# A graph network layer on one core: eight tiles that SyncE fetched row by row are gathered by GpSimd

## The chip, the cores and the metric

One core of a Trainium2 chip runs the whole kernel. The metric is the time of one execution on the device in microseconds, as the median of several runs. The engines are TensorE (PE, with its weight loads as PEld), VectorE (DVE), ScalarE (ACT), GpSimd (POOL) and SyncE (SP). A suffix q (SPq, DVEq) means the engine's sequencer: waits, register work and DMA issues.

## The reference

There are 12500 nodes with 128 features each and 400000 edges, sorted by destination. Cut to what matters:

```
rbf  = exp(-(distances[:, None] - centers)**2 / (2 * width**2))          # 50 centers up to 10.0
cut  = 0.5 * (cos(pi * distances / CUTOFF) + 1) * (distances <= CUTOFF)
W    = (silu(rbf @ fw1 + fb1) @ fw2 + fb2) * cut[:, None]                # per edge
messages = (h[src] @ pw + pb) * W
agg  = segment_sum(messages, dst)
y    = h + silu(agg @ mw1 + mb1) @ mw2 + mb2
out  = layernorm(x + y)
```

Edges longer than the cutoff of 10.0 contribute nothing, and most edges here are longer.

## The kernel before, in words

The program is written in the order in which it is to be issued: a manual schedule, in which a modelled clock decides how instructions of several activities are interleaved. Each engine works off its own instructions in that order, and waits on semaphores for its operands.

**Lists.** The edge list is cut into seven chunks of rows of 128 partitions. For each chunk VectorE shifts the near edges of a row to its front (`pack`, lines 508 to 512 and 502), puts them in lines (`columns`, L477 and L479), and GpSimd scatters the lines into a list `packed` in DRAM (L487). `unpack` reads the list back on SyncE (L805), separates sources, destinations and lengths (L823 to L853), transposes them on TensorE and copies the sources to `srci` (L891), one column for 128 edges. The lengths go to `near_d` in DRAM (L880).

**Quads.** The near edges make 139 quads of 512 edges, numbered q, each of four tiles of 128 edges, numbered j. QB gives the first quad of each chunk: 0, 13, 24, 46, 69, 91, 114. For each quad:

- `fetch` (L1026) gathers the projected rows `h[src] @ pw + pb`: one indirect DMA on GpSimd's queue per tile (L1032), 128 rows of 512 bytes, from the table `proj` in DRAM into a buffer `got`. The first 12 quads are gathered from `x` itself and projected afterwards, because `proj` isn't written yet.
- `radial` (L1046) loads the lengths of two quads on SyncE's queue, broadcast over the partitions (`d<-near_d`). ScalarE makes the radial basis of them (L1073, L1074), TensorE and ScalarE the first layer (`ph`, L1082; silu, L1088), TensorE the second (L1096, L1099).
- `message` (L1103) multiplies that with the gathered rows on VectorE (L1110). This is what gives the quad's buffer back.
- `place` (L1122) makes on VectorE a matrix that is the cutoff weight where an edge's destination meets a column; `sum_up` (L1142) multiplies it with the messages on TensorE, and `add` (L1165) adds the sums into `aggT` at the quad's base.

**Buffers.** There are 13 buffers `quad` and 8 buffers `x` for gathered rows, also used for other things. `place_of` gives each quad its buffer: at first all 21, from quad 63 on only nine, with ever fewer turns in between (at the end each buffer comes back after four quads). A gather waits until the message of the quad that had the buffer before is done.

**Gathers in order.** `fetches` (L435) puts gathers on GpSimd's queue as long as indices and buffers are there by the program's own model. It keeps a modelled time of GpSimd, `pool[0]`, and from it `there_at[q]`, when a quad will have landed; the modelled clock that paces the list-building (`pack_until`) goes by both.

**Single rows.** For the eight quads in `SINGLY` the first tile (j = 0) isn't gathered by GpSimd. `unpack` turns the sources into byte offsets, `at_row` (L905, once for each chunk that has such a quad), and appends 128 single rows per quad to a list `singles`. `one_by_one` (L1009), called once per quad of the main loop at L1470, issues some of these on SyncE's queue: a load of 32 offsets into registers (L1018), then for each row a plain DMA of 512 bytes (L1022) into `dl_0`, a keep tile with four places. `message` then takes the first tile from `dl_0` (L1108) and the other three from the gathered buffer (L1110), in two instructions:

```
            if j or q not in SINGLY:          # fetches, L442
                pool[0] += 1.29
...
            if q in SINGLY and j == 0:        # fetch, L1029
                continue
...
        if q in SINGLY and a == 0:            # message, L1106
            nc.vector.tensor_mul(msg[:, 0, :], pu_of[q][:, :H], alone.pop(q))
            a = 1
```

**Nodes.** From quad 70 on, finished columns of `aggT` go through the node layers (L1173 to L1176, L324, L327), the layer norm (L1192 to L1229) and out to DRAM (L170), in groups of node tiles set by quad number. The last groups come behind the last quad.

Of the kernel before, what the change touches and what calls it, by code (L numbers as in the profile page):

```python
# [65 lines left out]
CLEAR_C = 2  # L66
PACK_US = 1.5
EARLY_US = 7
SINGLY = (22, 45, 62, 67, 86, 102, 118, 133)
A_ROW = .58  # L70
AT_ONCE = 32
FROM_BANK = 3
# [8 lines left out]
def kernel(  # L81
# [342 lines left out]
    def before_it(q):  # L424

        return max((m for m in range(q) if place_of(m) == place_of(q)), default=-1)
# [8 lines left out]
    def fetches(until, most):  # L435

        while fetched[0] < QT * min(most, known[0]) and pool[0] <= until:
            q, j = divmod(fetched[0], QT)
            fetch(q, table=x if q < FROM_X else None, js=(j,))
            if j == 0:  # L440
                pool[0] = max(pool[0], summed.get(before_it(q), 0.0))
            if j or q not in SINGLY:  # L442
                pool[0] += 1.29
# [351 lines left out]
    def unpack(c):  # L795
# [105 lines left out]
        yield 0  # L901
        mine = [q for q in SINGLY if QB[c] <= q < QB[c + 1]]
        if mine:
# [105 lines left out]
    def one_by_one():  # L1009

        row_at[0] = max(row_at[0], clock[0] - 8.0)
        while singles and row_at[0] < clock[0]:
            row_at[0] += A_ROW
            q, e, i = singles.pop(0)
            if e == 0:
                alone[q] = dl_0[:, SINGLY.index(q) % 4, :]
            if e % AT_ONCE == 0:
# [8 lines left out]
    def fetch(q, idx=None, table=None, js=range(QT)):  # L1026
        got = quad_sb[place_of(q) if q >= 0 else 0]
        for j in js:
            if q in SINGLY and j == 0:  # L1029
                continue  # L1030
# [72 lines left out]
    def message(q, js=(0, QT)):  # L1103
        msg = own(q, "msg", 0)
        a, b = js
        if q in SINGLY and a == 0:  # L1106
            assert q in alone and all(s[0] != q for s in singles)
# [539 lines left out]
```

## Time and profile before

| | |
|---|---|
| median of 3 runs | 727.36 us (726.96 to 729.21) |
| the profiled execution | 731.18 us, of which the span in the trace 729.3 |
| TensorE, VectorE busy | 591.7 us (81%), 561.8 us (77%) |
| GpSimd, ScalarE busy | 532.4 us (73%), 402.7 us (55%) |
| DMA queues' share of 16 engines | q1 22.0%, q0 (GpSimd's) 19.6% |
| mean granted TensorE clock | 0.926 |

The profile is of one execution. Its page has the busy time of each engine, the span in 40 slices with the busy share in tenths, the chain of work that ended last, and the groups of instructions. A group's row has the source line, engine, operation, output<-inputs and the count, then busy us and mean ns of one, then the idle time of the engine just before these instructions with what ended it. "issue" there means that the engine waited for nothing that the profile shows. A row of the instructions in order of time has the start and the duration in us, then the instruction, and in brackets the idle time before it. A row of the waits has who waited for whom, the total in us, the number of times, and the longest. Busy time does not count register, semaphore and DMA-issuing instructions; for GpSimd's indirect DMAs the work of the engine itself is counted.

### The profile page before, as it was taken

To read this page: it belongs to the slowest core of one execution; us is meant where nothing else is said; L and a number is where in the kernel's file an instruction comes from. 1 tells how busy PE (TensorE), PEld (TensorE's weight loads), DVE (VectorE), ACT (ScalarE), POOL (GpSimd) and SP (SyncE) were. 2 spreads that over 40 slices of the span, in tenths; PEclk is the share of its full clock that TensorE was granted. 3 is DMA by queue.
4 is the path that set the end of the run, shared out by engine and by line. 5 is a ranking of instruction groups with operands and counts; after the bars stand their busy time and mean duration, and the time that the engine had idled before them with its cause. 6 is when DMAs were issued, how large, how long until landed. Compare 5 with 4: busy or idle time off the path is not lost.

```text
span 729.3 us, 13631 instructions
## 1 busy us (share of the span) xinstructions
PE 591.7 (81%) x3531; PEld 463.5 (64%) x3531; DVE 561.8 (77%) x1734; ACT 402.7 (55%) x572; POOL 532.4 (73%) x569
## 2 busy tenths in 40 slices
PE   6878777797888797888788979999977878887974
PEld 5767566576656676667466757777755656565752
DVE  8897998878968998989689959768555546564774
ACT  6547634275345864536347364839644744374584
POOL 6776777777777777777777777777777777777770
PEclk9998887999989998999889998999998989999998
DMA  8995443243234333242333343434433433445242
GB/s 262 326 314 182 124 134 87 68 145 90 87 100 140 86 96 106 84 141 81 88 99 121 104 105 114 147 116 142 126 99 113 139 99 98 112 125 149 55 139 69
DMA packets 53104, 91.38 MB, mean 125 GB/s; under 512 B 13824, under 2 KB 20576, under 8 KB 53018
## 3 DMA queue, kind: packets, MB, share of 16 engines
q1 hardware_dynamic: 34610, 53.34, 22.0%
q0 software_dynamic: 17840, 36.77, 19.6%
q8 instruction: 30, 0.49, 0.3%
q14 instruction: 56, 0.46, 0.2%
q10 hardware_dynamic: 568, 0.33, 0.2%
HBM read 74.59 MB, written 15.79 MB: 124 GB/s over the span
## 4 chain that ended last, share of the span: by engine, by line
DVE 25%; POOL 18%; PE 17%; issue 16%; DMA 15%; ACT 4%; DVEq 2%; SPq 1%; POOLq 0%; ACTq 0%
POOL quad L1032 14%; DMA quad<-proj,srci 7%; POOL x L1032 5%; DVE hot L1122 4%; PE bank L1099 4%; PE sums L1142 4%; PE ph L1082 3%; DVE aggT L1165 2%; DVE msg L1110 2%; PE bank L327 2%; DMA pair<-packed 2%; DVEq L1151 2%; DMA proj<-hp 2%; DVE r_d L502 2%; DVE quad L1122 2%
## 5 line engine op out<-in xcount | busy, mean ns | idle before, releaser
L1032 POOL DMA_INDIRECT quad<-proj,srci x421 | 400.5, 951 | 130.5 <-issue 104.9
L1099 PEld LDWEIGHTS bank<-fw_sb,s 128*128 128x128 f32 x1112 | 162.2, 210 | 67.5 <-issue 60.0
L1088 ACT ACTIVATE s<-ph 128x1024 f32<-128x1024 f32 x70 | 71.2, 1017 | 169.9 <-PE ph L1082 169.8
L1099 PE MATMUL bank<-fw_sb,s 128*128 128x128 f32 x1112 | 162.1, 293 | 0.0
L1082 PE MATMUL ph<-rbf,w_sb 102*128 102x512 f32 x278 | 141.1, 632 | 9.2 <-ACT rbf L1074 4.9
L1142 PEld LDWEIGHTS sums<-hot,msg 128*128 128x128 f32 x816 | 106.4, 196 | 55.2 <-DVE msg L1110 27.1
L1122 DVE TENSOR_SCALAR hot<-iota_n,dl,cut 128x80 f32<-128x80 f32 (+4 forms) x408 | 108.7, 343 | 24.8 <-PE sums L1142 22.0
L1142 PE MATMUL sums<-hot,msg 128*128 128x80 f32 (+4 forms) x816 | 109.5, 278 | 14.2 <-DVE msg L1110 13.9
L1096 PE MATMUL bank<-fb_b,ones_b 96*128 96x512 bf16 x139 | 56.8, 409 | 49.0 <-DVE msg L1110 24.5
L1032 POOL DMA_INDIRECT x<-proj,srci x79 | 75.3, 953 | 24.1 <-issue 20.7
L1110 DVE TENSOR_TENSOR msg<-bank,quad 128x512 f32<-128x512 f32 (+1 forms) x82 | 55.4, 676 | 41.6 <-DMA quad<-proj,srci 30.8
L1082 PEld LDWEIGHTS ph<-rbf,w_sb 102*128 102x128 f32 x278 | 50.5, 202 | 47.4 <-issue 36.7
L1165 DVE TENSOR_TENSOR aggT<-aggT,sums 128x80 f32 (+4 forms) x209 | 53.7, 257 | 27.4 <-PE sums L1142 10.7
L1073 ACT ACTIVATE rbf<-d,rbf_bias,rbf_scale 102x512 f32<-102x512 f32 x70 | 56.2, 803 | 26.5 <-DMA d<-near_d 26.4
L1032 POOL DMA_INDIRECT quad<-in_x_dram,srci x48 | 47.0, 979 | 18.7 <-issue 14.7
L327 PEld LDWEIGHTS bank<-pw_sb,xT 128*128 128x128 f32 (+1 forms) x292 | 43.5, 215 | 11.3 <-ACT xT L968 5.0
L1088 ACT ACT_TABLE_LOAD x36 | 46.2, 1283 | 0.6
L1074 ACT ACT_TABLE_LOAD x35 | 44.9, 1283 | 0.6
L327 PE MATMUL bank<-pw_sb,xT 128*128 128x128 f32 (+1 forms) x292 | 44.5, 301 | 0.8 <-ACT xT L968 0.6
L1074 ACT ACTIVATE rbf<-rbf 102x512 f32<-102x512 f32 x70 | 44.1, 630 | 1.5
L1142 PE MATMUL sums<-quad,quad 128*128 128x128 f32 (+3 forms) x296 | 42.4, 290 | 2.2 <-DVE quad L1110 1.9
L1110 DVE TENSOR_TENSOR quad<-bank,quad 128x512 f32<-128x512 f32 (+2 forms) x40 | 25.1, 631 | 24.3 <-DMA quad<-proj,srci 20.4
(268 smaller groups left out, 809.9 us busy)
## 6 DMA issues: line engine op xcount, KB each, us to landing
d<-near_d SPq DMA_DIRECT2D x70, 256.0 KB
dl<-proj SPq DMA_DIRECT2D x1024, 0.5 KB
x<-in_x_dram SPq DMA_DIRECT2D x46, 256.0 KB
quad<-proj,srci POOLq DMA_INDIRECT x421
proj<-hp SPq DMA_DIRECT2D x24, 256.0 KB
out_dram<-x SPq DMA_DIRECT2D x22, 256.0 KB
r_d<-in_edge_weight_dram SPq DMA_DIRECT2D x5, 256.0 KB
r_dst<-in_dst_dram SPq DMA_DIRECT2D x5, 256.0 KB
```

The source lines that it names most:

```text
L327: nc.tensor.matmul(to[:m, k, :], lT[:, k * P:k * P + m], w, start=False, stop=(k == a + c - 1))
L1032: nc.gpsimd.indirect_dma_start(out=got[:, j, :], out_offset=None, in_=proj if table is None else table, in_offset=bass.IndirectOffsetOnAxi ...
L1073: nc.scalar.activation(rbf[:u], d[:u], AF.Square, bias=rbf_bias[:u], scale=rbf_scale[:u])
L1074: nc.scalar.activation(rbf[:u], rbf[:u], AF.Exp, scale=-1.0 / (2.0 * width * width))
L1082: nc.tensor.matmul(ph[:, h, :], w1_sb[:2 * KR, h, :], rbf[:2 * KR], start=True, stop=True)
L1088: nc.scalar.activation(s[:, :n], ph[:, :n], AF.Silu)
L1096: nc.tensor.matmul(pu, ones_b[:, :P], bias_b["fb2"].rearrange("k j f -> k (j f)"), start=True, stop=False)
L1099: nc.tensor.matmul(pu[:, j * H:(j + 1) * H], s[:, j * P:(j + 1) * P], fw2_sb, start=False, stop=(j == QT - 1))
L1110: nc.vector.tensor_mul(msg[:, a:b, :], pu_of[q].rearrange("p (j f) -> p j f", j=QT)[:, a:b, :], got_of[q][:, a:b, :])
L1122: nc.vector.tensor_scalar(hot[:, j, :wide(q)], iota_n[:, :wide(q)], dl[:, at[0], at[1]], cut[:, at[0], at[1]], op0=OP.is_equal, op1=OP.mult)
L1142: nc.tensor.matmul(pa[:, k * W:k * W + wide(q)], msg[:, j, :], hot[:, j, :wide(q)], start=(j % n == 0), stop=(j % n == n - 1))
L1165: nc.vector.tensor_add(to, to, pa[:, k * W:k * W + wide(q)])
```

## The change

The tuple of quads whose first tile comes by single rows is emptied:

```
-SINGLY = (22, 45, 62, 67, 86, 102, 118, 133)
+SINGLY = ()
```

All 556 tiles are then gathered by GpSimd. `singles` stays empty, so `one_by_one` issues nothing, `at_row` isn't computed, and each message is one instruction. Since `fetches` counts 1.29 for each of the eight tiles more, the modelled times `pool[0]` and `there_at` grow, and the list-building instructions of the later chunks stand at somewhat other places between the quads.

## Prediction

> **What bounds the kernel now.** I read the page's shares of the span first, then the groups of GpSimd (POOL), its instructions in order of time, and last the messages of VectorE (DVE), which consume what GpSimd gathers.
>
> ```profile
> span 729.3 us, 13631 instructions
> ...
> POOL 6776777777777777777777777777777777777770
> ...
> DVE 25%; POOL 18%; PE 17%; issue 16%; DMA 15%; ACT 4%; DVEq 2%; SPq 1%; POOLq 0%; ACTq 0%
> ```
>
> By shares nothing is full: the chain that ended last passes over five engines, and GpSimd is never busier than seven tenths. But its row is the same digit from the second slice to the last but one. An engine that waits for others has an uneven row; this one looks like an engine that is always at it and loses a fixed share between its instructions. The groups of GpSimd (busy us, mean ns | idle us just before them) say so:
>
> ```profile
> L1032 POOL DMA_INDIRECT quad<-proj,srci x421 | 400.5, 951 | 130.5 <-issue 104.9 <-DVE aggT L1165 6.4 <-DMA quad<-proj,srci 5.2
> L1032 POOL DMA_INDIRECT x<-proj,srci x79 | 75.3, 953 | 24.1 <-issue 20.7 <-DMA x<-proj,srci 0.9 <-DVE aggT L1165 0.6
> L1032 POOL DMA_INDIRECT quad<-in_x_dram,srci x48 | 47.0, 979 | 18.7 <-issue 14.7 <-DVE srci L539 2.4 <-DMA proj<-hp 0.6
> L487 POOL DMA_INDIRECT packed<-line,at_i x7 | 7.0, 998 | 2.7 <-issue 1.5 <-DVE base_i L624 0.9 <-DVE aggT L1165 0.3
> ```
>
> There are 421 + 79 + 48 = 548 gathers and 7 scatters. Their idle time adds up to 130.5 + 24.1 + 18.7 + 2.7 = 176.0 us, or 0.317 us before each of the 555. In order of time (start, duration, what, idle before it) nearly every one has 0.30 or 0.31; those with more, and some that I need as marks, are:
>
> ```profile
> 7.11 1.21 POOL L1032 DMA_INDIRECT quad<-in_x_dram,srci  x1 [2.41 <-DVE srci L539]
> ...
> 71.38 0.94 POOL L1032 DMA_INDIRECT quad<-in_x_dram,srci  x1 [2.25 <-issue]
> ...
> 133.68 0.94 POOL L1032 DMA_INDIRECT quad<-proj,srci  x1 [0.30 <-issue]
> 136.37 0.94 POOL L1032 DMA_INDIRECT quad<-proj,srci  x1 [1.74 <-DVE at_row L905]
> ...
> 489.43 0.94 POOL L1032 DMA_INDIRECT quad<-proj,srci  x1 [1.08 <-DVE quad L1110]
> ...
> 549.40 0.94 POOL L1032 DMA_INDIRECT quad<-proj,srci  x1 [0.30 <-issue]
> ...
> 649.40 0.94 POOL L1032 DMA_INDIRECT quad<-proj,srci  x1 [0.30 <-issue]
> ...
> 668.22 0.94 POOL L1032 DMA_INDIRECT quad<-proj,srci  x1 [0.30 <-issue]
> ...
> 709.49 0.94 POOL L1032 DMA_INDIRECT quad<-proj,srci  x1 [0.30 <-issue]
> ```
>
> From 7.11 to 709.49 us GpSimd issues one gather behind the other. From 668.22 to 709.49 there are 33 steps: 41.27 / 33 = 1.2506 us each (0.94 of work, 0.30 between). Past its start it waited three times: 2.25 - 0.30 = 1.95 us at 71.38, 1.44 at 136.37, 0.78 at 489.43. That is all.
>
> Does the end follow from the last gather? I gave each gather its quad (a group of 512 edges) by counting, four to a quad and three where the quad is in SINGLY, and put the quad's message, the VectorE product that consumes it, beside its last gather. Quads 45, 97 and 134:
>
> ```profile
> 245.81 0.94 POOL L1032 DMA_INDIRECT quad<-proj,srci  x1 [0.30 <-issue]
> 291.97 0.55 DVE L1110 TENSOR_TENSOR msg<-bank,quad 128x384 f32<-128x384 f32 x1
> 508.15 0.94 POOL L1032 DMA_INDIRECT quad<-proj,srci  x1 [0.30 <-issue]
> 510.90 0.69 DVE L1110 TENSOR_TENSOR msg<-bank,quad 128x512 f32<-128x512 f32 x1 [1.47 <-PE bank L1099]
> 689.45 0.95 POOL L1032 DMA_INDIRECT quad<-proj,srci  x1 [0.30 <-issue]
> 692.97 0.69 DVE L1110 TENSOR_TENSOR quad<-bank,quad 128x512 f32<-128x512 f32 x1 [1.31 <-DMA quad<-proj,srci]
> ...
> 714.38 0.29 DVE L1110 TENSOR_TENSOR quad<-bank,quad 128x128 f32<-128x128 f32 x1 [0.76 <-issue]
> ```
>
> The lead of the gathers is 46.2 us at quad 45, 2.75 at quad 97, and stays near 3 up to quad 134, whose message waits for its data. VectorE's waits between 560 and 640 us (total, times, longest) show the same:
>
> ```profile
> DVE msg L1110 <- DMA quad<-proj,srci: 15.3, 6, 4.1
> DVE quad L1110 <- DMA quad<-proj,srci: 12.1, 8, 2.1
> ```
>
> So GpSimd has the stock, the consumer eats it up by about 505 us, and from there each message waits for GpSimd. Up to quad 134 **the gather queue sets the end**; the rest, from 692.97 to 729.3, is a tail of 36.3 us behind it.
>
> **The change part by part.** Eight quads lose their row-wise first tile. Removed on SyncE and VectorE:
>
> ```profile
> L1022 SPq DMA_DIRECT2D dl<-proj x1024: 224/228/405, 82.7 to 666.7; - x171
> L905 DVE TENSOR_SCALAR at_row<-f_src x6: 207/208/346, 79.9 to 445.3; 44x128 int32<-44x128 f32 x2, 46x128 int32<-46x128 f32 x2, 22x128 int32<-22x128 f32 x1, 54x128 int32<-54x128 f32 x1
> 685.72 0.29 DVE L1108 TENSOR_TENSOR msg<-bank,dl 128x128 f32<-128x128 f32 x1
> 687.08 0.56 DVE L1110 TENSOR_TENSOR msg<-bank,quad 128x384 f32<-128x384 f32 x1 [1.06 <-DMA quad<-proj,srci]
> ACT rbf L1073 <- DMA d<-near_d: 26.4, 9, 5.3
> ```
>
> - SyncE loses 1024 x 0.228 = 233 us of issuing. What stood behind the rows in its queue, the broadcast loads of the lengths (d<-near_d), goes out earlier, so up to 26.4 us of ScalarE's nine waits can go. VectorE loses 6 x 0.208 = 1.2 us and, with one product in place of two, 8 x (0.29 + 0.56 - 0.69) = 1.3 us. I count all this at nothing: the consumer before 505 us has a stock of gathers in front of it, and past 505 us it waits for GpSimd. Being earlier only lengthens those waits. If that cover were gone, it would be worth the second rival's price.
> - Added: 8 gathers, 548 becoming 556. All eight lie before quad 134, in GpSimd's queue ahead of everything that follows. Seven go in at 1.2506: **+8.75 us**.
> - The eighth, quad 22's, comes just before the wait at 136.37. GpSimd waits there for quad 24's indices, the first of the third list, written by this copy:
>
> ```profile
> 135.85 0.25 DVE L891 CAST srci<-bank 128x88 int32<-128x88 f32 x1 [0.42 <-PE bank L886]
> 488.47 0.69 DVE L1110 TENSOR_TENSOR quad<-bank,quad 128x512 f32<-128x512 f32 x1
> 422.94 0.29 DVE L479 TENSOR_TENSOR line<-r_d,bank 128x136 int32<-128x136 int32 x1
> 428.43 0.99 POOL L487 DMA_INDIRECT packed<-line,at_i  x1 [0.30 <-DVE aggT L1165]
> ```
>
>   The profile names at_row, the instruction right behind the copy, as the releaser; what the gather reads is srci. The queue stands still for 1.44 us, and a gather takes 1.25. It fits whole: **0**. If the indices came 1.4 us sooner it would cost 1.25.
> - The wait of 0.78 us at 489.43 is for a buffer (quad 94's), given back by quad 90's message of 488.47. Five added gathers lie ahead of it, of which four count: GpSimd gets there 5.0 us later and finds the buffer free, if that message is not 4.2 us later as well: **-0.78**.
> - Moved: the scheduler reckons GpSimd's time with 1.29 us for each gather, so the list-building instructions shift. In the changed program's order of instructions the last three scatters stand 0, 1 and 4 of the old gathers later in GpSimd's queue, and the index copies of the lists 0 to 3 messages later on VectorE. A scatter must not come before its lines: the tightest of these was ready at 423.23 and issued at 428.43, and now gets 8 gathers more ahead of it, so it waits for nothing. The last list's copy, at 445 before, is wanted by quad 114 at 588; 3 messages are some 12 us. Also nothing.
>
> Sum: 8.75 + 0 - 0.78 = **+8.0 us**. The profiled execution took 731.18 us (729.3 of span and 1.9 around it), so it would take 739.2. It lies 3.8 above the median of the runs, 727.36; on that median the forecast is **735.3 us**, 1.1% slower.
>
> The tail is taken over unchanged: the last message stands at 714.38, 4.9 us behind the last gather's start, where 2.75 was usual. There the consumer, not GpSimd, is late, by 4.9 - 2.75 = 2.1 us. If the relief of SyncE and ScalarE gave all of that back, the time would be 733.2, and 732.8 from the lowest of the runs, 726.96.
>
> **One rule of the Trainium skill weighed.** What a gather costs beside a busy VectorE is on these rows (all gathers into quads: shortest/median/longest ns; VectorE's busy us in two stretches):
>
> ```profile
> L1032 POOL DMA_INDIRECT quad<-proj,srci x421: 938/944/1344, 73.9 to 709.5; - x141
> 300.00:400.00 100.00, 88.39 (x248) 0.91 0.34 102
> 600.00:700.00 100.00, 61.13 (x205) 0.94 0.38 109
> ```
>
> Half the gathers take 944 ns or less although VectorE is busy for 88% of one stretch, and the worst takes 1344. If each added gather were a worst one, the price would grow by 8 x 0.40 = 3.2 us: 738.5. The Trainium skill, "SBUF — State Buffer", section "SBUF: two separate sides", says that a DMA issued from GpSimd starves while VectorE runs in a two-port mode, and its next section gives 620 ns alone against 3100 beside such a copy. That speaks against the change: by those figures eight gathers would cost an estimated 8 x 2.5 = 20 us more. This trace has no gather of that kind, so the sum goes by 944 ns.
>
> **The rivals.**
> 1. *Full price.* All eight gathers cost 1.25, because the waits at 136.37 and 489.43 move along with the lists and the messages: 8 x 1.2506 = 10.0, 737.4 us. For it: both waits are set by VectorE, whose order changes. Against: up to quad 22 only one 0.2 us instruction leaves VectorE, and VectorE has less to do by 489. 0.13.
> 2. *The consumer sets the pace* (other side: faster). Rows on SyncE hold back the length loads, ScalarE and then the messages; without them the messages come earlier, and the end with them. Price: at most the 26.4 us, 701 us. It decides only where GpSimd waits for buffers for longer than the 8 us added; it waited 0.78. 0.02.
> 3. *The rows slow the gathers* (no change). 1024 row transfers share the DMA engines with the gathers. Without them each gather might take its shortest, 938: busy time 522.8 us less 548 x 0.938 = 8.8 us, which pays for the whole change, 726.6. Against: from 549.40 to 649.40, with rows in flight, 80 steps take 1.2500; past the last row at 666.7 they take 1.2506. 0.03.
> 4. *Starved gathers*, the rule above: 738.5 by the worst row. 0.05.
> 5. *A shorter tail*, 733.2 as worked out: 0.07.
>
> That the change does something else is out: the changed program holds 556 gathers and no row transfer.
>
> **How the numbers follow.** The forecast, 734 to 736.5, gets the remaining 0.70. The range, 732.8 to 738.5, takes in the shorter tail, the full price and the worst row. A measurement of this kernel can tell about 0.3%, 2.2 us, from no change. Faster by more: rival 2, 0.02. Within: rival 3, 0.03. Slower: the rest, 0.95.
>
> **What would show it.** 556 gathers, again 1.25 us apart; the idle time before the first gather of quad 24 down from 1.74 to about 0.5, and no wait near 490; quad 134's last gather issued at 697.4 with its message still waiting for it; the last gather at 717.5; fewer waits of ScalarE for d, worth nothing. I am wrong if GpSimd shows waits of more than a microsecond behind quad 24, if the step is not 1.25, or if messages past quad 100 no longer wait for gathers.

## The result, and the profile after

The changed kernel takes 738.15 us in the median of 4 runs (736.08 to 739.7), the kernel before 728.29 in 4 runs on the same chip (726.96 to 730.58): a ratio of 1.0109, 95% interval 1.0073 to 1.0144, which is 7.9 us; the two medians themselves lie 9.9 us apart. Measured a second time, with other kernels beside it, it was 737.46 us against 730.51: 1.0085 (1.0056 to 1.0114), or 6.2 us, with 7.0 between the medians. So the change costs 6 to 10 us, about 1%; 8.0 had been forecast.

The page after, the busy line, GpSimd's row of the 40 slices and its largest group:

```profile
span 734.3 us, 11523 instructions
...
PE 590.1 (80%) x3531; PEld 463.1 (63%) x3531; DVE 560.6 (76%) x1720; ACT 403.9 (55%) x573; POOL 540.5 (74%) x577
...
POOL 6777777777777777777777777777777777777770
...
L1032 POOL DMA_INDIRECT quad<-proj,srci x428 | 407.4, 952 | 130.6 <-issue 104.5
```

GpSimd has 8 instructions and 8.1 us of busy time more (532.4 before) and the same flat row. The profiled execution took 736.08 us, 4.9 more than the one of before; it was the shortest of the four, and that of before, with 731.18, was longer than any of its four. In it, the first gather of quad 24 (start, duration, idle before), the last gather of quad 134 with its message, and the last gather of all:

```profile
134.12 0.94 POOL L1032 DMA_INDIRECT quad<-proj,srci  x1 [0.49 <-DVE part L910]
...
695.88 0.94 POOL L1032 DMA_INDIRECT quad<-proj,srci  x1 [0.30 <-issue]
698.93 0.69 DVE L1110 TENSOR_TENSOR quad<-bank,quad 128x512 f32<-128x512 f32 x1 [0.25 <-DMA quad<-proj,srci]
...
715.94 0.94 POOL L1032 DMA_INDIRECT quad<-proj,srci  x1 [0.30 <-issue]
```

In this execution the idle time before quad 24 has fallen from 1.74 to 0.49, with quad 22's gather ahead of it. No gather near 490 us waits any more. Between these gathers and their partners of before, the differences are -2.25 at quad 24 (134.12 - 136.37), +6.43 at quad 134 and +6.45 at the end. So the queue behind quad 24 became 8.7 us longer, and everything up to quad 24 ran 2.25 us earlier in this execution: it was 2.05 us ahead at quad 12 already, at 71.82 us, when no row transfer is out yet (the first of before is at 82.7). Behind the last gather 18.4 us are left (734.3 - 715.9), 19.8 before. Hence 8.7 - 2.25 - 1.45 = 5.0 in the span. The first of these three numbers belongs to the change, as the other runs show. The last does not: with the rows kept, the rest behind the last gather is as short (18.4 in the gathers alone). For the 2.25 no cause was found. The four kernels below without rows start quad 24 at 134.1 to 135.9 us and four with rows at 136.2 to 137.4; but among the latter is the one with only quad 22 moved, whose first row goes out at 138.4, and a kernel with ten quads by rows starts it at 133.4.

The waits of ScalarE and VectorE that SyncE's rows were suspected of (total, times, longest), from the waits of the changed kernel:

```profile
ACT rbf L1073 <- DMA d<-near_d: 3.2, 3, 1.6
DVE msg L1110 <- DMA quad<-proj,srci: 33.7, 15, 5.5
DVE quad L1110 <- DMA quad<-proj,srci: 27.9, 17, 3.6
```

ScalarE's waits for the length loads went from 26.4 us to 3.2. That is a real relief, and the kernel is slower. VectorE's waits for gathers went from 51.2 us to 61.6: what is gained ahead of a queue that sets the pace is spent waiting for it. Their rows in the kernel before:

```profile
DVE msg L1110 <- DMA quad<-proj,srci: 30.8, 15, 4.1
DVE quad L1110 <- DMA quad<-proj,srci: 20.4, 13, 2.5
```

### The profile page after: what moved, and what is told of

It is laid out like the page before. It is cut to its first block, busy times and chain, and to the rows that moved or that the text cites. A ratio compares the mean times of both kernels' runs of the same rounds, so it can differ in the third digit from the quotient of the medians.

```text
span 734.3 us, 11523 instructions
## 1 busy us (share of the span) xinstructions
PE 590.1 (80%) x3531; PEld 463.1 (63%) x3531; DVE 560.6 (76%) x1720; ACT 403.9 (55%) x573; POOL 540.5 (74%) x577
## 5 line engine op out<-in xcount | busy, mean ns | idle before, releaser
L1032 POOL DMA_INDIRECT quad<-proj,srci x428 | 407.4, 952 | 130.6 <-issue 104.5
L1082 PE MATMUL ph<-rbf,w_sb 102*128 102x512 f32 x278 | 142.8, 639 | 5.5 <-ACT rbf L1074 4.0
L1142 PEld LDWEIGHTS sums<-hot,msg 128*128 128x128 f32 x816 | 108.2, 199 | 54.4 <-issue 26.9
L1142 PE MATMUL sums<-hot,msg 128*128 128x80 f32 (+4 forms) x816 | 110.5, 280 | 14.5 <-DVE msg L1110 14.3
L1110 DVE TENSOR_TENSOR msg<-bank,quad 128x512 f32<-128x512 f32 x82 | 55.9, 681 | 39.0 <-DMA quad<-proj,srci 33.7
L1110 DVE TENSOR_TENSOR quad<-bank,quad 128x512 f32<-128x512 f32 (+1 forms) x40 | 25.9, 648 | 32.2 <-DMA quad<-proj,srci 27.9
```

The source lines that it names most:

```text
L1032: nc.gpsimd.indirect_dma_start(out=got[:, j, :], out_offset=None, in_=proj if table is None else table, in_offset=bass.IndirectOffsetOnAxi ...
L1082: nc.tensor.matmul(ph[:, h, :], w1_sb[:2 * KR, h, :], rbf[:2 * KR], start=True, stop=True)
L1110: nc.vector.tensor_mul(msg[:, a:b, :], pu_of[q].rearrange("p (j f) -> p j f", j=QT)[:, a:b, :], got_of[q][:, a:b, :])
L1142: nc.tensor.matmul(pa[:, k * W:k * W + wide(q)], msg[:, j, :], hot[:, j, :wide(q)], start=(j % n == 0), stop=(j % n == n - 1))
```

## The experiments

**The two halves of the change, each alone.** The first kernel adds the gathers and keeps the rows, which are still used; only the lines that skip the gather go:

```
-            if q in SINGLY and j == 0:
-                continue
```

> The kernel before with the eight first tiles gathered by GpSimd as well: the rows are still fetched by SyncE and still used, the order of everything else is that of before. Theory (GpSimd's queue sets the end): 556 gathers, seven of the eight added ones at 1.25 us, quad 22's hidden in the wait at 136 us, the buffer wait near 489 us gone: +8.0 us, ratio 1.011, the same as the change. Full price: +10.0, 1.0137. If SyncE's rows set the consumer's pace: the change's gathers cost more than its +8 to +10 and the removed rows give some back, so this kernel is slower than the changed one, above 740.

Measured: 737.15 us (6 runs) against 730.15, ratio 1.0096 (1.0067 to 1.0126). ScalarE's waits for d were 23.6 us, as before. Apart from the added gathers the instructions stand in the order of before, so it isn't the shifted list-building instructions that cost the time.

The second takes out the rows and adds no gather; in the first tile of the eight quads the message multiplies by ones, so that part of the result is left out:

```
 def one_by_one():
+    singles.clear()
...
-            nc.vector.tensor_mul(msg[:, 0, :], pu_of[q][:, :H], alone.pop(q))
+            nc.vector.tensor_mul(msg[:, 0, :], pu_of[q][:, :H], ones)
```

> The kernel before without the row transfers and their register loads on SyncE; the first tile of the eight quads isn't fetched by anyone, the message multiplies by a tile of ones instead (so this part of the result is left out). 548 gathers as before. Theory: no change, 0 to -1 us (the buffer wait of 0.78 at most goes), down to -2.9 if the tail gives back its lateness too; GpSimd's steps stay at 1.25. Consumer's pace: as much as ScalarE's waits for d, up to -26 us, ratio down to 0.965. Rows slow the gathers: -8.8 us, ratio 0.988, and a step shorter than 1.25.

Measured: 728.22 us (12 runs) against 730.15, ratio 0.9975 (0.9959 to 0.9991). So the added gathers are the whole cost (+7.0 us) and the removed rows give back between 0.7 and 3.0 us at best, not the 26 of the waits. ScalarE's waits for d fell to 14.3 us here, and VectorE's for gathers rose to 32.7 + 30.2 = 62.9: with no gather added, the relief is spent waiting. With gathers and without rows, the change itself was measured once more, on another chip and with the kernel before beside it:

> The changed kernel as it is, beside the others. Theory: +8.0 us on the kernel before, ratio 1.011, the same as with the rows kept (1.0096 measured there). If the rows' removal paid for something, it would lie below that, about 1.007.

Measured: 1.0085 (1.0056 to 1.0114). It can't be told from 1.0096, the gathers alone. The 0.0025 that the rows are worth by themselves is within what these intervals leave open, so whether a part of it survives in the changed kernel isn't settled.

**Is quad 22's gather free?** Once with only this one moved, once with the other seven:

```
-SINGLY = (22, 45, 62, 67, 86, 102, 118, 133)
+SINGLY = (45, 62, 67, 86, 102, 118, 133)     # e3
+SINGLY = (22,)                               # f4
```

> Only quad 22's first tile goes to GpSimd, the other seven stay with SyncE: 549 gathers. Theory: no change in time (within 0.3 us); in the profile the idle time before quad 24's first gather falls from 1.74 to about 0.5 and that gather starts no later relative to its neighbours. Full price: +1.25 us, ratio 1.0017, and the idle time there stays near 1.7.

> Seven of the eight first tiles go to GpSimd, quad 22's stays with SyncE: 555 gathers. Theory: the full change less a gather that was hidden, so the same time as the changed kernel: +8.0 us, ratio 1.011, with the wait of 1.4 us before quad 24's first gather as in the kernel before. If each added gather cost the same: 7/8 of the change's cost, 1.25 us less than the changed kernel.

Measured: 1.0011 (0.9988 to 1.0034) with only quad 22 moved, 1.0101 (1.0071 to 1.0132) with all but it: the time of the kernel before, and that of the changed one. One gather of 1.25 us is 0.17% and too small for these intervals; the profiles decide. First gather of quad 24, then any wait near 490, then the last gather, with only quad 22 moved:

```profile
136.16 0.94 POOL L1032 DMA_INDIRECT quad<-proj,srci  x1 [0.49 <-DVE at_row L905]
...
490.86 0.94 POOL L1032 DMA_INDIRECT quad<-proj,srci  x1 [2.73 <-DVE quad L1110]
...
710.93 0.94 POOL L1032 DMA_INDIRECT quad<-proj,srci  x1 [0.30 <-issue]
```

and with all but quad 22 moved:

```profile
137.43 0.94 POOL L1032 DMA_INDIRECT quad<-proj,srci  x1 [4.31 <-DVE part L910]
...
719.51 0.95 POOL L1032 DMA_INDIRECT quad<-proj,srci  x1 [0.30 <-issue]
```

With the gather the wait is 0.49 here, as in the first profile of the changed kernel, and without it 4.31. But this difference isn't the gather's alone. The second profile of the changed kernel, with the gather, has 1.73 there, as much as the kernel before without it, and the gathers alone have 2.37; first the one, then the other:

```profile
135.07 0.95 POOL L1032 DMA_INDIRECT quad<-proj,srci  x1 [1.73 <-DVE part L910]
```

```profile
137.12 0.94 POOL L1030 DMA_INDIRECT quad<-proj,srci  x1 [2.37 <-DVE at_row L905]
```

The wait is as long as it takes until the third list's indices are there, and that moment differs from one execution to the next: quad 24 starts at 134.12, 135.07, 136.16 and 137.12 us with quad 22's gather, and at 134.30, 136.37 and 137.43 without it. In each of these profiles GpSimd still waits there for longer than its usual 0.30, so the gather fits in ahead of the wait, twice with only 0.19 us to spare. GpSimd's row of gathers starts anew at that point: what stands ahead of it, an added gather or a late start, doesn't count as long as some of the wait is left; what stands behind it does.

**A double dose.** The changed kernel, with each of the eight gathers made once more, into a tile that nobody reads:

```
+            if q in AGAIN and j == 0:
+                nc.gpsimd.indirect_dma_start(
+                    out=dl_0[:, AGAIN.index(q) % 4, :], out_offset=None, in_=proj,
+                    in_offset=bass.IndirectOffsetOnAxis(ap=i, axis=0))
```

> The changed kernel with each of the eight added gathers made twice (the second into a tile nobody reads): 564 gathers. Theory: a linear price, again 1.25 us each, of which quad 22's finds only some 0.2 us of waiting left: +9.8 us on the changed kernel, ratio 1.0245 to the kernel before, and the messages past quad 97 or earlier wait for gathers. If the eight were partly hidden or the consumer set the pace: less than +6 on the changed kernel. If added gathers are starved by VectorE: more than +12.

Measured: 745.83 us (5 runs), ratio to the kernel before 1.0228 (1.0201 to 1.0254), so 16.6 us where 17.8 was expected. The price is about linear: in the table below the first seven gathers behind quad 24 add 8.7 us and the next seven 8.2. The same two marks in this kernel, and the group of the additional gathers:

```profile
135.93 0.94 POOL L1037 DMA_INDIRECT quad<-proj,srci  x1 [1.49 <-DVE part L911]
...
725.94 0.94 POOL L1037 DMA_INDIRECT quad<-proj,srci  x1 [0.30 <-issue]
```

```profile
L1034 POOL DMA_INDIRECT dl<-proj,srci x8 | 7.6, 947 | 2.4 <-issue 2.1 <-DMA quad<-proj,srci 0.3
```

Put together, from quad 24's first gather to the last of all, for each profiled execution (the rest of the span behind it in the last column):

| kernel | gathers added behind quad 24 | first to last, us | rest of the span |
|---|---|---|---|
| before | 0 | 573.1 | 19.8 |
| rows out | 0 | 573.5 | 18.5 |
| only quad 22 moved | 0 | 574.8 | 18.5 |
| gathers alone | 7 | 582.2 | 18.4 |
| all but quad 22 moved | 7 | 582.1 | 18.4 |
| changed | 7 | 581.8 | 18.4 |
| changed, again | 7 | 581.8 | 18.3 |
| double dose | 14 | 590.0 | 18.1 |

Three groups, and rows or no rows makes no difference in them. The 574.8 has its 1.7 us over 573.1 in the buffer wait at 490.86: 2.73 - 0.30 = 2.43 there, 0.78 in the kernel before.

**More rows in place of fewer.** If gathers are what costs, ten or twelve quads by single rows should be faster than eight. The modelled pace had to be quickened for the rows to fit:

```
-SINGLY = (22, 45, 62, 67, 86, 102, 118, 133)
-A_ROW = .58
+SINGLY = (22, 45, 62, 67, 86, 102, 110, 118, 126, 133)                 # f2
+A_ROW = .46
...
+SINGLY = (22, 34, 45, 56, 67, 78, 88, 98, 108, 118, 126, 133)          # f3
+A_ROW = .33
```

> Ten quads by single rows in place of eight, the two new ones late (22, 45, 62, 67, 86, 102, 110, 118, 126, 133), with the rows issued at a quicker modelled pace (A_ROW 0.46 in place of 0.58). 546 gathers. Theory: two gathers less behind quad 97, where every message waits for GpSimd: -2.5 us, ratio 0.9966. If SyncE's rows begin to hold back the consumer: 0 or slower, with messages past quad 100 no longer waiting for gathers.

> Twelve quads by single rows (22, 34, 45, 56, 67, 78, 88, 98, 108, 118, 126, 133), A_ROW 0.33. 544 gathers. Seven of them lie before quad 94 (five before), five behind it (three before). Theory with the buffer wait as a floor: GpSimd reaches quad 94 2.5 us sooner and only waits that much longer for its buffer, so the two early ones are lost and the two late ones gain: -2.5 us, ratio 0.9966, and a wait of some 3 us near 487. If only the count of gathers mattered: -5.0 us, 0.993, and no such wait. If the denser rows hold back the consumer: 0 or slower, waits of GpSimd for buffers of more than 4 us.

Measured: 767.34 us, 1.0493 (1.0458 to 1.0529), with ten, and 904.23 us, 1.2358 (1.2319 to 1.2397), with twelve. The expected -2.5 us didn't come: here the consumer falls behind, the rival that the runs with eight quads rule out there. Both the number of rows and the pace were changed, so these two runs don't tell which of them did it. The waits with ten quads, then with twelve:

```profile
ACT rbf L1073 <- DMA d<-near_d: 132.5, 31, 10.3
...
DVE two L823 <- DMA pair<-packed: 31.6, 5, 11.1
POOL quad L1032 <- DVE msg L1110: 25.3, 12, 9.6
```

```profile
ACT rbf L1073 <- DMA d<-near_d: 235.9, 39, 12.7
...
POOL quad L1032 <- DVE msg L1110: 113.5, 20, 17.7
...
DVE two L823 <- DMA pair<-packed: 60.1, 4, 23.2
```

What came late are the loads on SyncE's queue, which stand among the rows: the lengths (d) and the lists. And GpSimd, whose longest wait for a buffer in the kernel before was 1.1 us, now waits for them for 25.3 us with ten quads and 113.5 with twelve. A likely reason stands in SyncE's instructions in order of time, first with twelve quads, then in the kernel before:

```profile
505.58 12.78 SPq L1022 DMA_DIRECT2D dl<-proj  x31
518.55 0.37 SPq L170 DMA_DIRECT2D x<-in_x_dram  x1
519.02 0.53 SPq L1046 DMA_DIRECT2D d<-near_d  x1
519.66 11.34 SPq L1022 DMA_DIRECT2D dl<-proj  x26
```

```profile
513.95 3.74 SPq L1022 DMA_DIRECT2D dl<-proj  x9
...
522.07 8.29 SPq L1022 DMA_DIRECT2D dl<-proj  x17
```

One issue takes 228 ns in the median, but the stretch of 31 takes 12.78 us. A load of 32 offsets into registers is in it (L1018, 2.17 us at 510.6), so a row with what lies between costs 0.34 there; in the stretch of 17, which has such a load of 2.14 us too, 0.36, and in the nine rows without one 0.42. With its share of the load, 2.16 / 32 = 0.07, a row takes SyncE an estimated 0.41 to 0.49. At a modelled pace of 0.58 per row that leaves some room for its other work; at 0.46 little or none, at 0.33 less than none. That this is what held back the consumer is argued from these figures, not shown by a run of its own.

**An attempt to cure that.** Three kernels were to tell the pace from the count, and to take the length loads out of the rows' way: the pace alone (eight quads, A_ROW 0.46), the loads on ScalarE's queue with eight quads, and the same with ten, which was measured once more:

```
-        nc.sync.dma_start(d, v.to_broadcast([64, 2, QE]))
+        nc.scalar.dma_start(d, v.to_broadcast([64, 2, QE]))
```

> The kernel before with only the modelled pace of the rows changed, A_ROW 0.46 in place of 0.58: the same eight quads, 1024 rows and 548 gathers, but each quad's rows are put more densely among SyncE's other work. Theory: ten quads lost 37 us because rows really take some 0.4 us of SyncE each, so that at this pace the length loads behind them come late; then this kernel too is slower, by 5 to 30 us, with ScalarE's wait for d above 50 us (26.4 before). If only the number of rows mattered: no change.

> The kernel before with the length loads (d<-near_d) issued on ScalarE's queue in place of SyncE's; rows and gathers as before. Theory: GpSimd's queue sets the end, so 0 to -1 us, ScalarE's wait for d mostly gone. Rival: the 70 issues of 0.52 us are 36 us more of ScalarE's sequencer and delay the silu and with it the messages: slower by up to 36.

> Ten quads by single rows as in the earlier run (A_ROW 0.46, 546 gathers), but with the length loads on ScalarE's queue, out of the rows' way. Theory: the 37 us of that run came from the length loads behind the rows, so they go, and the two gathers less give -2.5 us against the kernel before, ratio 0.9966. If the rows hold back something else on SyncE (the lists' reads, the row transfers themselves): still slower than the kernel before by 10 us or more.

> The same kernel once more, beside a kernel before that takes its usual time: ten quads by single rows (A_ROW 0.46, 546 gathers), length loads on ScalarE's queue. Theory: the 37 us of the ten-quad run came from the length loads behind the rows in SyncE's queue; with these out of the way ScalarE hardly waits for d (132.5 us there), and two gathers less give -2.5 us, ratio 0.9966. If the rows hold back the lists' reads or the row transfers themselves instead: slower than the kernel before by 10 us or more, with VectorE waiting for the lists. If ScalarE's 70 issues of some 0.5 us cost it: slower, by up to 36 us, with GpSimd waiting for buffers.

All four ran on chips on which the kernel before itself took 1070 and 1071 us (three on one, the last on another), with a granted TensorE clock of 0.73 to 0.77 in their profiles (0.926 in the kernel before elsewhere), so they can't be set beside the runs above. Why these chips are so much slower isn't known. Against the same chip's kernel before, the ratios were 1.0268 (1.0111 to 1.0426) for the pace, 1.1137 (1.0925 to 1.135) for the loads on ScalarE, 1.2011 (1.1763 to 1.2259) for ten quads with them, and 1.2024 (1.1952 to 1.2096) for that once more. GpSimd waits long for buffers in all of them, least with the pace alone:

```profile
POOL quad L1032 <- DVE msg L1110: 134.3, 23, 20.0
```

So on such a chip denser rows cost something by themselves, and ScalarE's queue is the wrong place for the loads. How the loss with ten quads on a chip with the usual times divides into pace and count, and whether more than eight quads could pay there, stays open.

## Why the prediction was right, point by point

- **GpSimd's queue sets the end up to quad 134.** Right. One wait of GpSimd was left out of the working, 0.89 us at 32.23 before a scatter, far ahead of all that the change touches. From quad 24 to the last gather the profiles fall into three groups by the number of gathers there, with or without rows: seven more add 8.7 to 9.1 us, fourteen 16.9.
- **Seven gathers at 1.25, +8.75, less a buffer wait, -0.78.** Both terms are right; one of +0.8 is missing. From quad 24 to the end the queue grew by 8.7 us where 8.0 had been worked out. In the rows of the two profiles the buffer wait is gone, as forecast, but all the work of GpSimd behind quad 24 adds up to 440.7 us where it was 433.3: 7.4 more, of which seven gathers of 0.944 are 6.6. The other 0.8 are gathers that took longer than the usual 0.944; why there were more of them is open. The buffer wait itself differs between executions: it is 0.78 in the one of before, 2.43 in the one with only quad 22 moved, 0.38 at 487 (and 0.76 at 467) with the rows out. Seven added gathers eat up whatever it is, so this part of the cost differs with it.
- **735.3 us, most likely 734 to 736.5.** The forecast rested on a median of three runs, 727.36, and the kernel before was at 728.29 to 730.51 each time that it was measured beside others. The measured 738.15 lies inside the range but above those limits, nearer to the 737.4 of the full price: by this time alone, rival 1 would have looked better, and by the second measurement, with 7.0 us between the medians, worse. The forecast marks in the profile, 697.4 for quad 134's last gather and 717.5 for the last of all, were passed 1.5 and 1.6 us sooner: quad 24 started 2.25 us earlier, and the queue behind it grew by 0.7 more than forecast.
- **Quad 22's gather costs nothing.** Right, and for the reason given: with it GpSimd still waits at quad 24. The sign that was named for it, a wait down from 1.74 to about 0.5, is no good sign, though: it came true in the first profile and not in the second (1.73). Not seen: that the wait is a point where all executions start anew, and that its place differs by 3.3 us between them. That, and the tail, is why the two profiled executions differ by 5.0 us and not by 8.
- **What SyncE, ScalarE and VectorE lose is worth nothing.** Right to 0.25%: by itself it is worth 0.7 to 3.0 us. Where that comes from is open. It isn't saved behind quad 24: the profile with the rows out has 573.5 us from there to the last gather, 573.1 with them, and still has its buffer waits. That execution was ahead of the one of before by 2.07 us at quad 24 and had 1.3 us less behind the last gather, and neither could be tied to the rows.
- **The tail is taken over unchanged.** Right, in that the change doesn't touch it. The 19.8 us behind the last gather in the profile of before were that execution's; in seven others it is 18.1 to 18.5, with rows and without.
- **The rivals.** The full price, 1.0137, lies inside the interval of the first measurement (up to 1.0144), but above those of the changed kernel's second one, of the gathers alone and of all but quad 22; and its mechanism, that both waits move along, fails in the profiles: the buffer wait near 490 is gone wherever seven gathers were added, and quad 24 starts no later with quad 22's gather than without it. The consumer's pace as the bound of this change is out by the kernel with the rows removed (0.9975, not 0.965). That rows slow the gathers is out: 573.5 us from quad 24 to the end without rows, 573.1 with them. Starved gathers are out: the Trainium skill's figures ("SBUF — State Buffer", "A bandwidth-pool intuition that's wrong (but worth ruling out)") would make an estimated 20 us more of eight gathers, and the second eight measured 947 ns each. The shorter tail was no effect of the change.

## What to carry to other kernels

An engine can be the bound at 73% busy: look for a fixed idle time between its instructions and an even row in the slices, and count steps, not busy time. Price an added instruction by where the next real wait of its queue is: ahead of the wait it is free up to the wait's length, behind it it costs a full step to the end. And when another queue is used to unload the bound, its own limit may be close: here an estimated 0.4 to 0.5 us of SyncE for each row, and eight tiles by rows saved 1% where ten, at a denser pace, lost 5%.

## What the runs showed of the hardware

A gather of 128 rows of 512 bytes took GpSimd 1.25 us, 0.94 of work and 0.30 between, from 600 to 700 us of the kernel before, where VectorE was busy for 61% of the time, and 1.27 from 300 to 400, where it was busy for 88%; without the 1024 row transfers the steps in these stretches were 1.25 and 1.26. A row of 512 bytes issued by SyncE from register offsets took 228 ns in the median, and 0.34 to 0.42 us with what lay between two of them in the stretches shown, which I had not expected, besides a load of 32 offsets into registers of about 2.2 us. The loads of the kernel before (shortest/median/longest ns, first and last start in us):

```profile
L1018 SPq TENSOR_LOAD <-at_row x32: 2093/2160/2395, 80.2 to 649.7; - x32
```
